# An edge-attention layer on one core: sums head by head, and more neighbour rows fetched singly

## The chip, the cores and the metric

The kernel runs on one core of a Trainium2 chip. The metric is the device time of one execution in microseconds, the median of several runs; lower is better. Engines are named as in the profile: PE (TensorE, with PEld for its weight loads), DVE (VectorE), ACT (ScalarE), POOL (GpSimd) and SP (SyncE, which here only issues DMAs).

## What is computed

There are 12500 nodes with 128 features and 412500 edges, sorted by their target `dst`, each with 64 features of its own. Attention has 4 heads of 32.

```python
h = relu(layernorm(x))                       # (12500, 128)
hn = (h @ W_node.T).reshape(N, 4, 32)
e = (edge_attr_64 @ W_edge.T).reshape(E, 4, 32)
att = sum(concat([hn[src], hn[dst], e], -1) * a, -1)      # (E, 4)
att = where(att > 0, att, 0.2 * att)
m = maximum(segment_max(att, dst), 0.0)
ex = exp(att - m[dst])
denom = segment_sum(ex, dst) + (E - deg)[:, None] * exp(-m)
out = x + segment_sum((ex / denom[dst])[..., None] * hn[src], dst)
```

The data that the layer must move one by one are the rows `hn[src]`, one for each edge.

## The kernel before

**Tiles and batches.** Edges are cut into chunks of 896 (seven tiles of 128, one edge on each partition), and seven chunks make a batch: 49 tiles in each of NBT = 66 batches; the last one has six chunks, and its last chunk three tiles. An edge's number says which chunk it is in; the targets of a chunk span fewer than 32 nodes (W = 32), so what a chunk adds up fits 32 columns or partitions.

**Preparation.** The nodes are normalised and projected in units of XB = 9 blocks of 128, and written to a table in DRAM, one row of ROW = 144 float32 (576 bytes) for a node: four heads of AW = 35 (32 values, a one that becomes the sum of the weights, another one, and the head's logit) and four more. While the table isn't there yet, POOL gathers some tiles straight from `x` (L239), and the preparation treats these "raw" tiles as it treats nodes, so that they need no row of the table. `RAW = (49, 9)` says how many in batches 0 and 1. ACT also fills the accumulator `acc` there (L453).

**Fetching.** POOL issues one indirect DMA for each tile, 128 rows of the table into `hs` (L632), in order of batches. `hs` is one of RING = 3 buffers in turn. In iteration b POOL gathers batch b+1; ahead of it stands a small memset (L627) that waits until the sums of batch b-2 have read that buffer. Some tiles are left to other queues: `by_row(b)` tiles of batch b are loaded as 128 single rows each, whose addresses the engine first reads into registers, 32 at a time, and then issues one DMA for each row (`row_by_row`, L658). The last ACTROWS = 64 rows of a batch are issued by ACT two batches ahead, at the end of an iteration; SP issues the rest, SPROWS = 96 and more in an iteration, behind its other loads: `lw` (the target rows near a chunk, `load_near`), `eft` (the edge features, L572 and L573, two batches ahead) and the penalties between segments (`load_pen`).

```python
def by_row(b):
    return (2 if b % EVERY == 0 else 1) if LOOSE < b < NBT - 1 else 0   # EVERY = 4, LOOSE = 4
```

**One iteration.** Each engine's instructions run in the order in which the program writes them; nothing reorders them. Iteration b has these steps:

- `weigh(b)`, DVE with ACT for the exponential: waits until the rows of batch b have landed (`landed`, L666), adds the logits of source and target (L734), transposes them to 32 partitions of 896 edges (L736), adds the edge's logit `z` from PSUM (L739), takes the leaky relu (L742), then the maximum of each segment by a scan forward (L745) and one backward (L748), subtracts it (L749), exponentiates on ACT (L752) and turns the weights back (L756 to L760).
- `mark(b)`: one-hot of each edge's target within its chunk (L702 to L710), `hot`.
- `scatter(b)`: DVE multiplies the rows by their weights, chunk by chunk (L774), and PE adds them up.
- `spread(b+1)` on ACT (L590) and `choose(b+1)` on DVE (L594 to L607): the target's logit of each edge, chosen from 32 rows by the bits of its number.
- `begin(b+2)`: PE's product of edge features with the attention weights into `z` (L691).
- `collect` and `close` of batch b-1: ACT copies the sums out of PSUM into `r` (L823); every second batch `merge` joins the two batches' 14 chunks in one scan along the chunks, with the running maximum, and adds the result to `acc` (L829 to L869). The last ALONE = 4 batches are merged one by one. When a part of seven blocks of nodes is complete, `finish` divides by the denominator, adds `x` and writes it out (L942 to L965); its turning of columns into rows is done by small copies on ACT (L955), or, at the very end, by products with the identity on PE (L957).

**The sums.** They are taken in two groups of four chunks (the middle chunk's heads are split between the groups), each group one chain of seven products: the weights of the product are the one-hots of four chunks, 128x128, and the moving side is 502 consecutive floats of four chunks' rows.

```python
            for t in range(T):
                at = (t * CB + q0) * ROW + g * SPLIT
                scattered[s.b] = nc.tensor.matmul(pa, s.hot[:, t, q0:q0 + G, :]..., flat[:, at:at + RUN],
                                 start=(t == 0), stop=(t == T - 1))
```

Of each result only the blocks in which a chunk's one-hot meets its own rows are used, 32 partitions of 35 columns for a head; `collect` copies these 28 blocks of a batch one by one. The last batch, with six chunks, is summed chunk by chunk (`scatter_few`, L796), and the first steps of its `weigh` are done for the tiles 0 to 4 first (EARLY = 5) and then for the other two.

## Time and profile before

| | |
|---|---|
| runs | 4023.95, 4022.22, 4022.31 us; median 4022.31 |
| profiled execution | 4021.72 us, span 4019.9 us |
| mean granted clock of TensorE | 0.678 |
| busy: PE, PEld | 1455.8 us (36%), 570.9 us (14%) |
| busy: DVE | 2373.7 us (59%) |
| busy: ACT | 865.9 us (22%) |
| busy: POOL | 3010.7 us (75%) |
| moved by DMA | 418.03 MB, 104 GB/s on average |

The span is the time from the first to the last record of the profile; the execution's own time has 1.8 us more around it. "L632 POOL" names the source line and the engine of a group of instructions; "out<-in" are the names of the tiles that it writes and reads, followed by their shapes. In groups, "x3090" counts them, and the figures behind the bar are the busy time in us, the mean duration of one in ns, and the idle time of the engine ahead of them with what ended it. In the timeline a row begins with its start and its duration in us; "x28" at its end means that so many records in a row were joined. One product in float32 leaves two records on PE.

### The profile page before, as it was taken

Reading aid. Unit: us, or ns where it says so; the run is one execution under the profiler, and the core shown is the slowest. Engines: PE = TensorE matmul, PEld = TensorE weight load, DVE = VectorE, ACT = ScalarE, POOL = GpSimd, SP = SyncE. Lnnn points to the kernel's source line nnn. Section 1 sums busy time; section 2 is a strip of 40 time slices with the busy share of each in tenths; the row PEclk is TensorE's granted clock in tenths of the full one; section 3 lists DMA queues with packets and bytes.
Section 4 is the critical chain, followed back from the end, with each engine's and each line's share of the span. In section 5 each row is a group of like instructions: output and inputs, shape, how many; then the busy total and the mean of one; then the engine's idle time right before and its main releaser. Section 6 shows DMA issues by size and latency. Waiting matters only on the chain.

```text
span 4019.9 us, 40260 instructions
## 1 busy us (share of the span) xinstructions
PE 1455.8 (36%) x3485; PEld 570.9 (14%) x3485; DVE 2373.7 (59%) x4282; ACT 865.9 (22%) x2682; POOL 3010.7 (75%) x3224
## 2 busy tenths in 40 slices
PE   5652432432442442442342442342342342343342
PEld 4320110110110110110110111110111110111111
DVE  7895565565565565465565565566465456465466
ACT  6321122112122112112122112122122122122122
POOL 6777777777777777777777777777777777777774
PEclk9776666766666666666666766676776676676676
DMA  7443333433333433433433433433334333434331
GB/s 214 130 134 109 100 96 108 110 89 99 107 91 108 110 94 99 110 87 105 109 97 95 110 88 106 108 104 88 110 89 110 104 108 85 109 89 109 109 93 42
DMA packets 283438, 418.03 MB, mean 104 GB/s; under 512 B 81019, under 2 KB 199862, under 8 KB 283146
## 3 DMA queue, kind: packets, MB, share of 16 engines
q0 software_dynamic: 100736, 231.80, 22.4%
q1 hardware_dynamic: 161232, 173.91, 14.5%
q10 hardware_dynamic: 21178, 9.69, 1.0%
q14 instruction: 262, 2.15, 0.2%
q8 instruction: 30, 0.49, 0.1%
HBM read 399.60 MB, written 15.51 MB: 103 GB/s over the span
## 4 chain that ended last, share of the span: by engine, by line
POOL 66%; issue 22%; DVE 7%; PE 3%; DMA 1%; ACT 1%; POOLq 0%; DVEq 0%; SPq 0%; ACTq 0%
POOL hs L632 66%; PE pa L781 1%; DVE hs L774 1%; PE z L691 1%; DVE stats L335 1%; DMA hs<-table,ends 1%; DVE hT L381 1%; DVE pick L607 1%; DVE m L748 0%; DVE up L745 0%; DVE hot L710 0%; DVE a L739 0%; ACT both L752 0%; DVE z L742 0%; DVE a L749 0%
## 5 line engine op out<-in xcount | busy, mean ns | idle before, releaser
L632 POOL DMA_INDIRECT hs<-table,ends x3090 | 2946.6, 954 | 945.0 <-issue 933.4
L781 PE MATMUL pa<-hs,hot 128*128 128x502 f32 x1820 | 924.6, 672 | 2428.0 <-DVE hs L774 2428.0
L734 DVE TENSOR_TENSOR logits<-hs,pick 128x196 f32<-128x196 f32 (+1 forms) x67 | 32.9, 491 | 1349.4 <-DVEq L666 1349.2
L781 PEld LDWEIGHTS pa<-hs,hot 128*128 128x128 f32 x1820 | 395.8, 222 | 2948.9 <-issue 2892.3
L823 ACT COPY r<-pa 32x35 f32<-32x35 f32 x1820 | 379.7, 209 | 1531.0 <-issue 1204.4
L774 DVE TENSOR_TENSOR hs<-hs,exr 128x924 f32<-128x924 f32 x455 | 472.5, 1110 | 0.0
L691 PE MATMUL z<-eft,wa 128*32 128x512 f32 (+3 forms) x1056 | 436.5, 549 | 13.5 <-DMA eft<-in_ef 13.5
L752 ACT ACTIVATE both<-a 32x224 f32<-32x224 f32 x264 | 102.4, 388 | 1153.1 <-DVE a L749 1150.7
L607 DVE COPY_PREDICATED pick<-exr,lw 128x3136 f32<-128x3136 int32 x66 | 239.8, 3633 | 0.0
L607 DVE COPY_PREDICATED pick<-exr,pick 128x1568 f32<-128x1568 int32 (+3 forms) x198 | 230.6, 1165 | 6.8
L590 ACT COPY pick<-lw 128x3136 f32<-128x3136 f32 x66 | 184.8, 2800 | 2.7 <-ACTq L666 1.2
L869 DVE TENSOR_TENSOR acc<-acc,a 128x70 f32 x461 | 107.2, 233 | 70.0 <-issue 51.2
L691 PEld LDWEIGHTS z<-eft,wa 128*32 128x32 f32 (+1 forms) x1056 | 94.6, 109 | 358.0 <-issue 350.7
L745 DVE TENSOR_TENSOR_SCAN up<-pen_sb,z 32x896 f32<-32x896 f32 x66 | 132.6, 2010 | 2.3
L748 DVE TENSOR_TENSOR_SCAN m<-pen_sb,up 32x896 f32<-32x896 f32 x66 | 132.5, 2007 | 2.3
L710 DVE TENSOR_TENSOR hot<-exr,key 128x448 f32<-128x448 f32 (+1 forms) x260 | 129.0, 559 | 6.7
L739 DVE TENSOR_TENSOR a<-z,zst 32x224 f32<-32x224 f32 (+2 forms) x268 | 101.0, 377 | 12.6 <-PE z L691 2.7
L756 DVE SCALAR_TENSOR_TENSOR both<-pen_sb,m 32x224 f32<-32x224 f32 x264 | 100.2, 380 | 2.7
L955 ACT COPY up<-a 32x224 f32<-32x224 f32 (+1 forms) x224 | 74.5, 332 | 36.0 <-DVE a L947 29.3
L742 DVE SCALAR_TENSOR_TENSOR z<-a 32x896 f32<-32x896 f32 (+1 forms) x67 | 72.1, 1076 | 2.3
L749 DVE TENSOR_TENSOR a<-z,m 32x896 f32<-32x896 f32 x66 | 71.3, 1080 | 2.3
L239 POOL DMA_INDIRECT hs<-in_x,ends x58 | 54.9, 947 | 18.1 <-issue 17.4
(166 smaller groups left out, 991.3 us busy)
## 6 DMA issues: line engine op xcount, KB each, us to landing
hs<-table SPq DMA_DIRECT2D x5760, 0.6 KB
eft<-in_ef SPq DMA_DIRECT2D x66, 1344.0 KB
hs<-table ACTq DMA_DIRECT2D x3840, 0.6 KB
hs<-table,ends POOLq DMA_INDIRECT x3090, 2.5
lw<-near SPq DMA_DIRECT2D x461, 64.0 KB
eft<-in_ef SPq DMA_DIRECT2D x66, 224.0 KB
pen_sb<-pens SPq DMA_DIRECT2D x66, 98.1 KB
table<-rows ACTq DMA_DIRECT2D x9, 648.0 KB
```

The costliest lines, as they stand in the source:

```text
L590: nc.scalar.copy(pick[:, :, :s.chunks, :], lw[:, None, :s.chunks, :n].to_broadcast([P, T, s.chunks, n]))
L607: nc.vector.copy_predicated(pick[:, :, :s.chunks, :n], bit[:, :, :, None].to_broadcast([P, T, s.chunks, n]), more)
L632: load = nc.gpsimd.indirect_dma_start(out=s.hs[:n, t * CB + q, :], out_offset=None, in_=table[:, :], in_offset=bass.IndirectOffsetOnAxis(a ...
L691: s.made = own_half(s, nc.tensor.matmul(s.z[:, part], wa3[:n, j, :], s.eft[:n, j, part], start=(j == 0), stop=(j == SB - 1)))
L710: nc.vector.tensor_tensor(s.hot[:, :, q0:q0 + n, :].rearrange("p t q r -> p q t r"), rows_ps[:, None, None, :].to_broadcast([P, n, T, W]), ...
L745: on_half(s, nc.vector.tensor_tensor_scan(up[:, e0:e1], s.pen[:, e0:e1], z, up[:, e0 - 1:e0] if e0 else 0.0, op0=OP.add, op1=OP.max))
L748: nc.vector.tensor_tensor_scan(m[:, ::-1], s.pen[:, CE:0:-1], up[:, ::-1], 0.0, op0=OP.add, op1=OP.max)
L752: nc.scalar.activation(both[g * R:(g + 1) * R, 0, :, :], grouped(att, g), AF.Exp)
L774: nc.vector.tensor_tensor(rows, rows, ex_ps[:, :, q * H:(q + 1) * H, None].to_broadcast([P, T, H, HB]), op=OP.mult)
L781: scattered[s.b] = nc.tensor.matmul(pa, s.hot[:, t, q0:q0 + G, :].rearrange("p q r -> p (q r)"), flat[:, at:at + RUN], start=(t == 0), sto ...
L823: nc.scalar.copy(to, pa[row:row + W, k:k + AW])
L869: nc.vector.tensor_tensor(cols, cols, put[:, i0 + i, :, :], op=OP.add)
```

## The change

It consists of six parts.

1. **Sums head by head.** `add_up` forms, for each chunk, tile and head, a product of its own: the chunk's one-hot (128x32) as weights, the 35 columns of the head as the moving side, into the 32 partitions of that head (`tile_position`) and the 35 columns of that chunk. All sums of a batch then lie in one tile of 128x245, and `collect` is one copy on ACT.
2. **DVE's steps.** `weigh_part` writes L739's sum to `up` in PSUM, makes the leaky relu out of two steps (0.2 times it into `att`, then the maximum of the two), and gives the product of the weights `up` in place of `m`. `merge` keeps `scale` and `put` in PSUM.
3. **Raw tiles.** Batch 1 gets 18 in place of 9, 67 in all. They are no longer part of the preparation: `measure_late` and `rows_late` normalise and project them in the loop, ahead of and within iteration 0. The filling of `acc` moves to iteration 1.
4. **Tiles by rows.** `by_row` gives one tile in every fourth batch and two in the others, from batch 3 to the last; ACT issues 80 or 120 rows in parts spread over its iteration (`act_some`), and SP puts 64 rows ahead of its other loads and 50 or more behind them.
5. **The last batch in two parts.** `end_in_parts` weighs, multiplies and adds up the tiles 0 to 3 of all chunks and then the tiles 4 to 6 as two segments of a chunk, which the merge joins as twelve columns.
6. **Order.** `finish` always turns by products on PE; the last batches are collected and closed in their own iteration; `mark` of the next batch comes earlier there.

```diff
-EARLY = 5
+EARLY = 4
-LOOSE = 4
-RAW = (T * CB, XB)
+LOOSE = 2
+RAW = (T * CB, 2 * XB)
-RUN = (G - 1) * ROW + SPLIT
+RUN = 512
-SPROWS = 96
-ACTROWS = 64
+SPROWS = 114
+FRONT = 64
+ACTROWS = (80, 120)
+MIDDLE = 16
+WHILE = 24

 def by_row(b):
-    return (2 if b % EVERY == 0 else 1) if LOOSE < b < NBT - 1 else 0
+    return (1 if b % EVERY == 1 else 2) if LOOSE < b < NBT else 0
+
+def act_rows(b):
+    n = ACTROWS[by_row(b) - 1] if by_row(b) else 0
+    return n if b < NBT - 2 else n * 3 // 4 if b < NBT - 1 else n // 2
...
+    def act_some(b, n):
+        if b < NBT:
+            n = min(n, batch(b).by_act)
+            batch(b).by_act -= n
+            row_by_row(batch(b), nc.scalar, ENG.Activation, n)
...
+    def weigh_part(s, t0, t1, before):
...
         for g in range(NQT):
-                on_half(s, nc.vector.tensor_tensor(grouped(att, g)[:, t0:t1, :], grouped(s.z, g)[:, t0:t1, :],
-                                                   zst[g * R:(g + 1) * R, t0:t1, :], op=OP.add))
+            on_half(s, nc.vector.tensor_tensor(grouped(up, g), grouped(s.z, g),
+                                               zst[g * R:(g + 1) * R, t0:t1, :], op=OP.add))
-            on_half(s, nc.vector.scalar_tensor_tensor(z, att[:, e0:e1], 0.2, att[:, e0:e1], op0=OP.mult, op1=OP.max))
+        nc.vector.tensor_scalar(att[:, e0:e1], up[:, e0:e1], 0.2, None, op0=OP.mult)
+        on_half(s, nc.vector.tensor_tensor(z, up[:, e0:e1], att[:, e0:e1], op=OP.max))
...
         for g in range(NQT):
             nc.vector.scalar_tensor_tensor(both[g * R:(g + 1) * R, 1, t0:t1, :], grouped(s.pen[:, 1:], g), -1.0 / BIG,
-                                           grouped(m, g), op0=OP.mult, op1=OP.mult)
+                                           grouped(up, g), op0=OP.mult, op1=OP.mult)
...
+    def add_up(s, pa, q, t0, t1):
+        for t in range(t0, t1):
+            for h in range(H):
+                scattered[s.b] = nc.tensor.matmul(
+                    pa[h * W:(h + 1) * W, q * AW:(q + 1) * AW], s.hot[:, t, q, :],
+                    s.hs[:, t * CB + q, h * AW:(h + 1) * AW],
+                    start=(t == t0), stop=(t == t1 - 1), tile_position=(0, h * W))
+
     def scatter(s):
...
+        for q in range(CB):
+            multiply(s, q, 0, T)
+            add_up(s, pa, q, 0, T)
...
     def collect(s):
...
+        nc.scalar.copy(merged[first][0][:, :, at:at + CB], s.sums)
...
+        measure_late(batch(1))
         for b in range(NBT - 1):
...
+            if b:
+                front = FRONT - row_by_row(batch(b + 1), nc.sync, ENG.SP, FRONT)
             load_near(batch(b + 1))
...
             if b:
-                more = max(SPROWS, batch(b + 1).left)
+                more = max(SPROWS - front, batch(b + 1).left)
                 more = row_by_row(batch(b + 1), nc.sync, ENG.SP, more)
                 if b + 2 < NBT:
-                    row_by_row(batch(b + 2), nc.sync, ENG.SP, min(more, max(0, batch(b + 2).left - ACTROWS)))
+                    row_by_row(batch(b + 2), nc.sync, ENG.SP, min(more, max(0, batch(b + 2).left - act_rows(b + 2))))
             weigh(s, before)
...
             scatter(s)
+            if b == 0:
+                rows_late(batch(1))
             spread(batch(b + 1))
+            act_some(b + 2, MIDDLE)
             if before:
-                close(before, b)
+                close(before, b + 2)
...
+            if b == 1:
+                nc.scalar.copy(acc.rearrange("p q d -> p (q d)"), carry_m.to_broadcast([P, NQ * AW]))
...
             if b + 2 < NBT:
                 clear_rows(batch(b + 2))
-                row_by_row(batch(b + 2), nc.scalar, ENG.Activation, ACTROWS)
+                act_some(b + 2, P)
```

`close` issues WHILE = 24 of ACT's rows between the merge and the finish of a part (`act_some(coming, WHILE)`). The functions left out of the diff are `measure_late` and `rows_late` (statistics, scaling on ACT and DVE, transposes and products with the projection on PE, a copy on ACT, for three tiles at a time) and `end_in_parts`.

More of the change, by code (lines that the diff above doesn't have):

```diff
@@ L452, in chunk_ranges @@
         def chunk_ranges():
-            nc.scalar.copy(acc.rearrange("p q d -> p (q d)"), carry_m.to_broadcast([P, NQ * AW]))
             for g in range(NG):
@@ L784, in scatter_few @@
-    def scatter_few(s, by_chunk):
-        for q in range(s.chunks):
-            rows = by_chunk[:, q, :, :].rearrange("p t (h k) -> p t h k", h=H)[:, :, :, :HB]
-            nc.vector.tensor_tensor(
-                rows, rows, ex_ps[:, :, q * H:(q + 1) * H, None].to_broadcast([P, T, H, HB]), op=OP.mult)
-            if q % G == 0:
-                pa = ps.tile([P, RUN], F32, name="pa", bufs=3)
-                s.sums.append(pa)
-            at = q % G * W
-            held = tiles_of(s.c0 + q)
-            for t in range(held):
-                nc.tensor.matmul(pa[at:at + W, :EROW], s.hot[:, t, q, :], s.hs[:, t * CB + q, :EROW],
-                                 start=(t == 0), stop=(t == held - 1), tile_position=(0, at))
+        open_weights(s)
@@ L825, in merge @@
-    def merge(c0, n, r):
+            r = work.tile([P, AW * (MC + 1)], F32, name="r")
+            merged[first] = r[:, :AW * (n + 1)].rearrange("p (d c) -> p d c", d=AW),
+        at = 1 + s.c0 - chunk_of(first)
+        nc.scalar.copy(merged[first][0][:, :, at:at + CB], s.sums)
+    def merge(c0, count, r, breaks=None):
+        n = count if breaks is None else 2 * count
+        step = n // count
+        breaks = new[:, c0:c0 + n] if breaks is None else breaks.rearrange("p c k -> p (c k)")
@@ L987, in close @@
             return
-        merge(chunk_of(first), chunks_of(first, last), merged.pop(first))
+        merge(chunk_of(first), chunks_of(first, last), *merged.pop(first))
+        if any(behind == last for _, _, behind in parts()):
+            act_some(coming, WHILE)
         for b0, n, behind in parts():
             if behind == last:
-                stores.append(finish(work, ps, "up", em_ps, b0, n, now + 1 < NBT))
+                stores.append(finish(work, ps, "up", em_ps, b0, n))
     with tc.manual_schedule():
@@ L1061 @@
                 held_x[b0] = load_part(work, b0, n)
-        for g in range(2):
-            collect(before, g)
-        weigh(s, None)
-        scatter(s)
-        close(before, NBT - 2)
-        for g in range(2):
-            collect(s, g)
-        close(s, NBT - 1)
+        merged[s.b] = end_in_parts(s)
+        close(s)
         for store in stores:
```

256 lines of the change are left out of this document (155 added, 101 removed).

## The prediction

> **What bounds the kernel now.** I read the page first, then POOL's own line, the waits, and stretches of the timeline at the start, in the middle and at the end.
>
> ```profile
> span 4019.9 us, 40260 instructions
> ...
> PE 1455.8 (36%) x3485; PEld 570.9 (14%) x3485; DVE 2373.7 (59%) x4282; ACT 865.9 (22%) x2682; POOL 3010.7 (75%) x3224
> ...
> POOL 66%; issue 22%; DVE 7%; PE 3%; DMA 1%; ACT 1%; POOLq 0%; DVEq 0%; SPq 0%; ACTq 0%
> ...
> L632 POOL DMA_INDIRECT hs<-table,ends x3090 | 2946.6, 954 | 945.0 <-issue 933.4
> ...
> L823 ACT COPY r<-pa 32x35 f32<-32x35 f32 x1820 | 379.7, 209 | 1531.0 <-issue 1204.4
> ...
> L752 ACT ACTIVATE both<-a 32x224 f32<-32x224 f32 x264 | 102.4, 388 | 1153.1 <-DVE a L749 1150.7
> ...
> L590 ACT COPY pick<-lw 128x3136 f32<-128x3136 f32 x66 | 184.8, 2800 | 2.7 <-ACTq L666 1.2
> ```
>
> POOL is busy for 75% of the span and, with the pauses called issue, makes 88% of the chain that ended last. Nearly all of it is one line, L632: 3090 gathers of 128 rows. DVE (59%), PE and ACT are far from full.
>
> ```profile
> L632 POOL DMA_INDIRECT hs<-table,ends x3090: 938/944/1822, 85.4 to 3973.5; - x194
> ```
> ```profile
> DVE logits L734 <- DVEq L666: 1349.2, 62, 29.1
> ...
> POOL hs L632 <- issue: 933.4, 3083, 0.3
> ```
>
> The first row gives POOL's pace: (3973.5 - 85.4) / 3089 = 1.259 us from gather to gather. Its median is 0.944 us, yet 2946.6 us of busy time over 3090 makes 0.954: 2946.6 - 3090 x 0.944 = 29.6 us are gathers that something held up, so an undisturbed one takes 1.259 - 0.0096 = 1.249 us. The pauses before them never exceed 0.3 us: POOL waits for nobody between 85 and 3974 us. DVE on the other hand waits 1349 us at L734 for rows, some 20 us in each of 66 batches. So the time is 85 us of start, 3090 gathers one behind the other, and a tail of 46 us.
>
> **POOL's gathers.** From the code: a batch in which by_row gives k leaves 49 - k tiles to POOL. Before, LOOSE = 4 and batches 5 to 64 give 45 x 1 + 15 x 2 = 75 tiles; after, batches 3 to 65 give 16 x 1 + 47 x 2 = 110. RAW's second entry goes from 9 to 18, so nine more tiles come from x before the table exists. POOL's gathers from the table fall from 3090 to 3046: 44 x 1.249 = 55.0 us.
>
> **The held gathers.** One batch from the middle:
>
> ```profile
> 2007.83 1.09 DVE L742 SCALAR_TENSOR_TENSOR z<-a 32x896 f32<-32x896 f32 x1
> ...
> 2008.55 1.19 POOL L632 DMA_INDIRECT hs<-table,ends  x1 [0.30 <-issue]
> ...
> 2014.05 1.56 DVE L756 SCALAR_TENSOR_TENSOR both<-pen_sb,m 32x224 f32<-32x224 f32 x4
> ...
> 2015.03 1.01 POOL L632 DMA_INDIRECT hs<-table,ends  x1 [0.30 <-issue]
> ...
> 2019.61 7.27 DVE L774 TENSOR_TENSOR hs<-hs,exr 128x924 f32<-128x924 f32 x7
> ...
> 2024.06 14.96 PE L781 MATMUL pa<-hs,hot 128*128 128x502 f32 x28 [35.84 <-DVE hs L774]
> ...
> 2030.45 24.14 ACTq L658 DMA_DIRECT2D hs<-table  x64
> ...
> 2033.14 1.83 DVE L869 TENSOR_TENSOR acc<-acc,a 128x70 f32 x7
> 2033.84 0.94 POOL L632 DMA_INDIRECT hs<-table,ends  x1 [0.31 <-issue]
> ...
> 2038.94 6.55 PE L691 MATMUL z<-eft,wa 128*32 128x512 f32 x16
> ```
>
> The gather that begins at 2008.55, while L742 runs, takes 1.19 us (+0.25), the one beside L756 1.01 (+0.07): 0.31 us in a batch, 20 us in 65 batches, of the 29.6. Both steps read two SBUF tiles; L749, L745 and L774, with z, up or ex_ps in PSUM, leave no such mark. The change puts a into PSUM as up, splits L742 into a product and a maximum with one SBUF input each, and gives L756 up in place of m. I take 22 us of the 29.6 to go (the ends are 0 and 29.6): 7.6 stay, L734 and the last copy_predicated keeping two SBUF inputs. The Trainium skill (SBUF — State Buffer, Who interferes with whom) says that a DVE instruction with two SBUF inputs contends with a GpSimd instruction that reads SBUF and that one with at most one does not; the trace agrees for L742 (1.19 us) but not for the short L869 (two inputs, 0.94 us beside it), and by the rule alone the sum would be up to 7.6 us less than by my count.
>
> **PE.** A full batch goes from 14 products of 128x502 (28 records, 14.96 us above) to 7 x 7 x 4 = 196 of 32x35, two records each: 392. Nothing of that shape is in the trace. The nearest rows:
>
> ```profile
> 4009.07 1.94 PE L957 MATMUL up<-a,ident 128*32 128x128 f32 x32 [12.01 <-DVE a L947]
> ```
> ```profile
> L796 PE MATMUL pa<-hs,eft 128*32 128x140 f32 x76 | 9.3, 337 | 26.2 <-DVE hs L788 26.2
> ```
>
> L957 has the same four column positions, with 128 columns: 1.94 / 32 = 61 ns a record, so 392 take 23.9 us at most by it, and 392 x 35/128 x 61 ns = 6.5 us if only columns count. L796 uses one position at a time and 140 columns: 9.3 / 76 = 122 ns, or 48 us. I take 12, since the positions do alternate; DVE feeds them in 7.3 us anyway. With 6.55 us for z (L691) even the dearest row gives 54.5 us against POOL's 47 x 1.249 = 58.7 in a batch, so PE stays hidden, and hs of batch b is not overwritten for two batches more. The Trainium skill (TensorEngine Tiling (Array Packing), Instruction Overhead) speaks against such small products: some 60 cycles each, whatever the columns. As an estimate from that page, with the 2.4 GHz of the Trainium skill's TensorE: Matmul & The Clock Gate (its first table), 392 x 60 cycles are 9.8 us; no run here shows it, and by it as by my 12 PE stays hidden and the sum is the same.
>
> **ACT and SP.** ACT loses 28 copies of 0.209 us for one of 128x245 (0.4 us, by the form of L590, 2800 ns for 3136), and the finish's copies by ACT, now on PE. It issues 120 rows in a two-tile batch instead of 64. 24.14 / 64 = 0.377 us a row makes 45.2 us; with L752 (102.4 / 66 = 1.6), L590 2.8, the copy 0.4 and a merge's two steps about 0.8 it is 51 of 58.7 us. The groups are smaller, which may cost up to 5 us more. SP issues about 114 rows for 93, by the same 0.377 us 43 us; 64 of them now stand ahead of lw and eft in its queue, which are wanted a batch later, so DVE's 20 us of slack hide that. The added DVE step, about 1.1 us by L742, is hidden by the same slack; if ACT or PE used it up, POOL would stand still only after another batch.
>
> **The start.**
>
> ```profile
> 74.67 0.94 POOL L239 DMA_INDIRECT hs<-in_x,ends  x1 [0.30 <-issue]
> 85.41 0.94 POOL L632 DMA_INDIRECT hs<-table,ends  x1 [9.80 <-DMA table<-rows]
> ```
> ```profile
> 86.19 11.63 ACT L453 COPY acc<-carry_m 128x13720 f32<-128x13720 f32 x1
> ```
> ```profile
> 181.81 12.05 PE L781 MATMUL pa<-hs,hot 128*128 128x502 f32 x28 [1.69 <-DVE hs L774]
> ```
> ```profile
> 199.60 0.12 POOL L627 MEMSET gate<- 128x1 f32 x1
> ```
>
> Nine more raw gathers end the raw ones at 74.67 + 9 x 1.249 = 85.9; the first from the table follows at 87.2 instead of 85.4 (+1.8). Batch 1 is left with 31, so the gate for batch 3, now at 199.6, comes at 87.2 + 80 x 1.249 + 3 = 190, and needs scatter(0), now done at 193.9. The preparation ends about 9 us earlier (three units fewer, some 4.5 us, and ACT's 11.6 us fill of acc moves to batch 1, of which I count 5), weigh(0) gains measure_late and one step, about 4 us: scatter(0) ends near 188 to 194. Then rows_late, ACT's fill and its first 120 rows (together 60 us ahead of batch 2's exp) bring scatter(2) to 300 to 322 against a gate at 307. I take 3 us of waiting on POOL in all (ends 0 and 15).
>
> **The tail.** From the rows of batch 64 on:
>
> ```profile
> 3928.51 0.50 DVE L734 TENSOR_TENSOR logits<-hs,pick 128x196 f32<-128x196 f32 x1 [18.97 <-DVEq L666]
> ...
> 3940.34 0.20 DVE L702 TENSOR_SCALAR dk<-ends 128x49 int32<-128x49 int32 x1
> ...
> 3942.87 7.27 DVE L774 TENSOR_TENSOR hs<-hs,exr 128x924 f32<-128x924 f32 x7
> ...
> 3963.78 0.20 DVE L594 TENSOR_TENSOR away<-ends,floor 128x49 int32<-128x49 int32 x1
> ...
> 3973.38 0.23 DVE L734 TENSOR_TENSOR logits<-hs,pick 128x120 f32<-128x120 f32 x1
> 3973.46 0.95 POOL L632 DMA_INDIRECT hs<-table,ends  x1 [0.31 <-issue]
> ...
> 3977.63 0.20 DVE L734 TENSOR_TENSOR logits<-hs,pick 128x48 f32<-128x48 f32 x1
> ...
> 3986.35 6.25 DVE L788 TENSOR_TENSOR hs<-hs,exr 128x924 f32<-128x924 f32 x6
> ...
> 3992.56 0.19 DVE L832 COPY run<-carry_m 128x1 f32<-128x1 f32 x1
> ...
> 3998.81 0.19 DVE L832 COPY run<-carry_m 128x1 f32<-128x1 f32 x1
> ...
> 4007.21 0.17 DVE L942 TENSOR_SCALAR rest<-acc 128x16 f32<-128x16 f32 x1
> ...
> 4011.84 0.39 SPq L965 DMA_DIRECT2D out<-xg  x1
> ```
>
> Count from E, the end of POOL's last gather (before: 3974.4, end of span E + 45.5). Batch 65 has 37 gathers by POOL, so L734 of batch 64 stands at E - 44.6. Then weigh 11.8 + 1.1, products 7.3, choose and mark of batch 65 9.6 (3963.78 to 3973.38): E - 14.8. The sums of batch 64 are there by E - 10 even at 61 ns, and its merge (6.3, from one L832 at 3992.56 to the next at 3998.81) ends near E - 5. The last batch's five-tile first steps took 4.25 us, the two-tile ones and the rest from 3977.63 to 3986.35 8.7 us: a part of four tiles costs about 8.8 us and 3.9 of products, one of three 7.6 and 2.6. E + 18; PE and one copy 2; merge of twelve columns 6.7; finish 4007.21 to 4011.84, 4.6; write and end 8.1. The span ends at E + 39.4, a gain of 6 us (ends 3 and 9).
>
> **Sum.** Last gather starts at 87.2 + 3045 x 1.249 + 7.6 + 3 = 3901.0, E = 3902.0, span 3941.4. The profiled execution took 4021.7 us for a span of 4019.9, so 3943.2; the median of the runs is 0.6 above it: 3944 us.
>
> **Rivals.** (1) The held gathers stay held, because something other than the second SBUF input holds them or the new steps fall at the same moment: +22 us, 3966. For it: L734 and L607 keep two SBUF inputs and their place shifts. Against it: L749 and L774 leave no mark. (2) The rows come late: if ACT's cycle in a two-tile batch passes 58.7 us, DVE waits at L734 for them. One us over, in 47 batches, is 47 us: 3991. Against it: one-tile batches with 80 rows give back 15 us each, and DVE has slack. (3) Slower: PE becomes the bound. If a record costs over (58.7 - 6.55) / 392 = 133 ns, scatter no longer fits. With a weight load in series at each record (570.9 / 3485 = 0.164 us by the page's PEld) a batch takes 392 x 0.164 + 6.55 = 70.8 us: 12.1 over in 47 batches and 10.9 in the others, about 4700; at 140 ns 2.7 over, 4071. Against it: 122 ns on one position alone, 61 on four. (4) The rows that replace gathers slow the other gathers, so that nothing is won: 55 / 3046 = 18 ns each would do, about 4000. Against it: gathers under ACT's and SP's rows take 0.94 us like the others.
>
> **Chances.** Forecast 0.79, (1) 0.08, (2) 0.04, (3) 0.06, (4) 0.03. A measurement of this kernel tells about 0.2% (8 us) from no change. All but (3) and a corner of (2) and (4) are faster: faster 0.90, same 0.03, slower 0.07. The range goes from 3930 (no wait in the start, no held gather, tail at its better end) to 3966 (rival 1, which is also the forecast with 15 us of waits in the start and the worse tail).
>
> **What would show it.** In the profile after: L643 x3046 with a mean near 0.946 us and first start near 87; no long gather beside the weigh steps; POOL's pauses still 0.3 us but for a few between 190 and 370 us; PE's sums of one batch between 7 and 24 us; DVE still waiting for rows in each batch; the last gather near 3901. The forecast is wrong if POOL's idle time grows by tens of us, if the new gathers' median is over 0.95, or if PE's sums pass 52 us a batch.

## The result, and the profile after

The changed kernel takes 3987.71 us (median of 4 runs, 3983.86 to 3989.80) against 4022.26 us for the kernel before: 0.9913 of it, 95% interval 0.9895 to 0.9930. It is faster by 0.9%, 34.5 us where 78 were forecast, and 3987.7 lies above the range of 3930 to 3966. The profiled execution took 3983.86 us for a span of 3982.1.

The page of the changed kernel, its first lines, the chain that ended last, and the groups that answer to those shown of before:

```profile
span 3982.1 us, 96155 instructions
...
PE 1116.7 (28%) x27848; PEld 633.4 (16%) x27848; DVE 2457.0 (62%) x4386; ACT 433.7 (11%) x693; POOL 2953.8 (74%) x3189
...
ACTq 50%; DVE 13%; SPq 13%; issue 12%; DMA 3%; ACT 3%; DVEq 0%; PE 0%
...
L643 POOL DMA_INDIRECT hs<-table,ends x3046 | 2881.1, 946 | 928.1 <-issue 919.6
L832 PE MATMUL pa<-hs,hot 128*32 128x35 f32 x25480 | 486.4, 241 | 2526.1 <-DVE hs L825 1518.2
...
L781 DVE STREAM_TRANSPOSE exr<-both 128x224 f32<-128x224 f32 (+1 forms) x67 | 28.3, 423 | 1023.9 <-ACT both L775 1023.7
```

POOL's line is what was forecast: 3046 gathers with a mean of 946 ns. But POOL is no longer in the chain that ended last. Half of that chain is ACT's queue (ACTq: the loading of row addresses and the issuing of DMAs, which don't count as busy), and the largest idle time of DVE no longer stands at the first step of a batch, where it waited for rows (L734 before, L760 now), but at L781, where it waits for ACT's exponential: 1023.7 us in 65 batches. For rows DVE waits only 1.4 us in all.

Where POOL's gathers began and ended, and POOL's and DVE's waits in the changed kernel:

```profile
L643 POOL DMA_INDIRECT hs<-table,ends x3046: 938/944/1791, 87.0 to 3910.2; - x191
```
```profile
POOL gate L638 <- PE pa L832: 8.3, 1, 8.3
POOL hs L643 <- DVE hs L631: 5.2, 1, 5.2
```
```profile
DVE exr L781 <- ACT both L775: 1023.7, 65, 29.1
...
DVE logits L760 <- DVEq L684: 1.4, 5, 0.5
```

The last gather starts at 3910.2 us and ends at 3911.2. The span ends 70.9 us after that; before, 45.5. So of the 40.7 us between the forecast's span (3941.4) and the measured one, 9.2 lie ahead of the last gather (POOL waits 8.3 us at 315 us and 5.2 us at 3885 us where 3 were counted; the gathers and the first start came out about 2 us better) and 31.5 behind it. In the timeline at the end:

```profile
3910.24 0.94 POOL L643 DMA_INDIRECT hs<-table,ends  x1 [0.30 <-issue]
...
3910.54 2.84 SPq L591 DMA_DIRECT2D lw<-near  x6
...
3917.09 2.43 ACT L600 COPY pick<-lw 128x2688 f32<-128x2688 f32 x1 [20.04 <-ACTq L684]
...
3919.55 3.13 DVE L617 COPY_PREDICATED pick<-exr,lw 128x2688 f32<-128x2688 int32 x1 [13.35 <-ACT pick L600]
...
3936.23 0.32 DVE L760 TENSOR_TENSOR logits<-hs,pick 128x96 f32<-128x96 f32 x1 [0.20 <-DVEq L684]
...
3961.01 0.36 ACT L800 COPY r<-pa 128x210 f32<-128x210 f32 x1 [5.41 <-DVE pa L815]
```

The first step of the last batch (L760 at 3936.23) begins 25 us after the end of POOL's last gather. It waited for nothing that POOL does: SP came to the loads of `lw` for this batch only at 3910.54, behind 64 single rows, DVE stood still for 13.35 us until ACT had spread what they bring (L617 behind L600), and only then could it finish with the batch before. What follows takes as long as forecast. DVE had been behind, by more or by less, all along. This is the time from the end of the last gather of a batch to the batch's first step on DVE, in us, counted from the traces (the n-th gather, with n from `by_row` and RAW); the kernels of the lower rows are those of the experiments below:

| batch | 3 | 10 | 20 | 30 | 40 | 50 | 60 | 65 |
|---|---|---|---|---|---|---|---|---|
| before | 6 | 2 | 2 | 2 | 2 | 2 | 2 | -1 |
| after | 83 | 48 | 45 | 29 | 29 | 16 | 12 | 25 |
| SPROWS = 116 (e1_fours) | 84 | 30 | 10 | 8 | 3 | 10 | 5 | -4 |
| WHILE = 0 (e2_no_while) | 83 | 55 | 63 | 52 | 55 | 60 | 68 | 12 |
| 118 tiles by rows (g5_seven_of_eight) | 84 | 45 | 46 | 55 | 55 | 39 | 52 | 24 |

A batch takes POOL 59.1 us on average, and DVE 58.25 us in the changed kernel (batches 20 to 60, from one L760 to the next). So from batch 10 on the lag of the start is worked off by less than 1 us in a batch. It goes up and down on the way (6 us at batch 57, 27 at 59, 8 at 61), and over the last four batches, which are merged one by one, it rises once more, to 33 us at batch 63; 25 are there at the end, where nothing hides them. How much of these 25 us is left from the start and how much is new isn't separated.

What holds DVE shows in ACT's timeline. Two stretches, the first of the changed kernel, the second of the same with SPROWS = 116:

```profile
2021.94 1.59 ACT L775 ACTIVATE both<-a 32x224 f32<-32x224 f32 x4 [30.82 <-issue]
...
2035.56 0.56 ACT L878 ACTIVATE up<-dif 128x462 f32<-128x462 f32 x1 [8.94 <-DVE dif L876]
...
2043.30 52.54 ACTq L669 DMA_DIRECT2D hs<-table  x104
2095.89 1.59 ACT L775 ACTIVATE both<-a 32x224 f32<-32x224 f32 x4 [59.55 <-issue]
```
```profile
2041.84 49.37 ACTq L669 DMA_DIRECT2D hs<-table  x119
2098.92 1.59 ACT L775 ACTIVATE both<-a 32x224 f32<-32x224 f32 x4 [54.69 <-DVE a L773]
```

In the first, 104 rows take 52.54 us (0.505 us a row), and the exponential follows at once, at 2095.89. DVE's own timeline of the same stretch:

```profile
2069.88 1.08 DVE L773 TENSOR_TENSOR a<-z,m 32x896 f32<-32x896 f32 x1
...
2097.51 0.43 DVE L781 STREAM_TRANSPOSE exr<-both 128x224 f32<-128x224 f32 x1 [24.96 <-ACT both L775]
```

It had the input ready at 2070.96 and stood still for 24.96 us. In the second 119 rows take 49.37 us (0.415 a row), and it is ACT that waits for DVE ("<-DVE a L773"). The chain of the changed kernel names what fills the first stretch:

```profile
2036.34 6.84 ACTq L665
...
2054.18 7.06 ACTq L665
...
2072.63 7.13 ACTq L665
```

L665 is the register load of row addresses ahead of a group of rows. Before the change they took about 2.2 us for 32 addresses; here three in a row take 7. The groups by line, before (L654) and after (L665), minimum, median and maximum in ns:

```profile
L654 ACTq TENSOR_LOAD <-shared x120: 2140/2224/3551, 279.4 to 3863.0; - x120
```
```profile
L665 ACTq TENSOR_LOAD <-shared x297: 765/2282/7439, 228.1 to 3880.9; - x149
L665 SPq TENSOR_LOAD <-shared x284: 917/2190/7172, 217.6 to 3913.7; - x142
```

### The profile page after: what moved, and what is told of

Its sections match the earlier page's. It is cut to its first block, busy times and chain, and to the rows that moved or that the text cites. A ratio compares the mean times of both kernels' runs of the same rounds, so it can differ in the third digit from the quotient of the medians.

```text
span 3982.1 us, 96155 instructions
## 1 busy us (share of the span) xinstructions
PE 1116.7 (28%) x27848; PEld 633.4 (16%) x27848; DVE 2457.0 (62%) x4386; ACT 433.7 (11%) x693; POOL 2953.8 (74%) x3189
## 4 chain that ended last, share of the span: by engine, by line
ACTq 50%; DVE 13%; SPq 13%; issue 12%; DMA 3%; ACT 3%; DVEq 0%; PE 0%
ACTq L669 34%; ACTq L665 16%; SPq L669 7%; DVE hs L825 6%; SPq L665 5%; DMA lw<-near 3%; DVE hot L728 2%; DVE pick L617 1%; ACT both L775 1%; SPq L591 1%; ACT pick L600 1%; DVE acc L905 1%; SPq L587 1%; ACT up L878 0%; DVE up L896 0%
## 5 line engine op out<-in xcount | busy, mean ns | idle before, releaser
L643 POOL DMA_INDIRECT hs<-table,ends x3046 | 2881.1, 946 | 928.1 <-issue 919.6
L832 PE MATMUL pa<-hs,hot 128*32 128x35 f32 x25480 | 486.4, 241 | 2526.1 <-DVE hs L825 1518.2
L832 PEld LDWEIGHTS pa<-hs,hot 128*32 128x32 f32 x25480 | 424.1, 146 | 2624.0 <-issue 2525.1
L781 DVE STREAM_TRANSPOSE exr<-both 128x224 f32<-128x224 f32 (+1 forms) x67 | 28.3, 423 | 1023.9 <-ACT both L775 1023.7
L825 DVE TENSOR_TENSOR hs<-hs,exr 128x924 f32<-128x924 f32 (+2 forms) x466 | 478.4, 1097 | 0.0
L775 ACT ACTIVATE both<-a 32x224 f32<-32x224 f32 (+2 forms) x268 | 103.1, 385 | 2826.6 <-issue 2729.2
L617 DVE COPY_PREDICATED pick<-exr,lw 128x3136 f32<-128x3136 int32 x66 | 240.9, 3650 | 15.2 <-ACT pick L600 15.2
L617 DVE COPY_PREDICATED pick<-exr,pick 128x1568 f32<-128x1568 int32 (+3 forms) x198 | 230.4, 1164 | 6.8
L770 DVE TENSOR_TENSOR_SCAN up<-pen_sb,z 32x896 f32<-32x896 f32 (+1 forms) x67 | 133.4, 1990 | 121.8 <-DMA pen_sb<-pens 120.6
L600 ACT COPY pick<-lw 128x3136 f32<-128x3136 f32 x66 | 184.7, 2798 | 83.9 <-ACTq L684 83.6
L905 DVE TENSOR_TENSOR acc<-acc,up 128x70 f32 x461 | 105.1, 228 | 90.2 <-issue 55.5
L772 DVE TENSOR_TENSOR_SCAN m<-pen_sb,up 32x896 f32<-32x896 f32 (+1 forms) x67 | 132.6, 1979 | 2.3
L765 DVE TENSOR_TENSOR up<-z,zst 32x224 f32<-32x224 f32 (+2 forms) x268 | 103.3, 385 | 12.8
L779 DVE SCALAR_TENSOR_TENSOR both<-pen_sb,up 32x224 f32<-32x224 f32 (+2 forms) x268 | 100.0, 373 | 3.8
L769 DVE TENSOR_TENSOR z<-up,a 32x896 f32<-32x896 f32 (+1 forms) x67 | 72.0, 1075 | 2.3
L773 DVE TENSOR_TENSOR a<-z,m 32x896 f32<-32x896 f32 (+1 forms) x67 | 71.4, 1066 | 2.3
```

Of the source, the lines that this page charges most:

```text
L600: nc.scalar.copy(pick[:, :, :s.chunks, :], lw[:, None, :s.chunks, :n].to_broadcast([P, T, s.chunks, n]))
L617: nc.vector.copy_predicated(pick[:, :, :s.chunks, :n], bit[:, :, :, None].to_broadcast([P, T, s.chunks, n]), more)
L643: load = nc.gpsimd.indirect_dma_start(out=s.hs[:n, t * CB + q, :], out_offset=None, in_=table[:, :], in_offset=bass.IndirectOffsetOnAxis(a ...
L770: on_half(s, nc.vector.tensor_tensor_scan(up[:, e0:e1], s.pen[:, e0:e1], z, 0.0, op0=OP.add, op1=OP.max))
L775: nc.scalar.activation(both[g * R:(g + 1) * R, 0, t0:t1, :], grouped(att, g), AF.Exp)
L825: nc.vector.tensor_tensor(rows, rows, ex_ps[:, t0:t1, q * H:(q + 1) * H, None].to_broadcast([P, t1 - t0, H, HB]), op=OP.mult)
```

## The experiments

The theory (A) after this: the loads that take 7 us start at a place in the list of addresses that is not a multiple of four. SPROWS = 114 leaves such places, since 114 is 2 more than a multiple of four while the other sizes are multiples of it, but for ACT's shares of the last two batches. Sorting ACT's 297 and SP's 284 loads by where they start: 32 addresses take 2.06 to 3.08 us from a multiple of four and 6.66 to 7.44 us from elsewhere; 16 take 1.2 and 3.6 to 3.9; for 32 that is 0.072 and 0.226 us an address. The rivals were (B) that the rows which ACT issues between a merge and a finish (WHILE) hold up DVE, and (C) that DVE's own work is too long to work off the start.

**e1_fours.** All sizes multiples of four.

```diff
-SPROWS = 114
+SPROWS = 116
```

> The changed kernel with SPROWS = 116 in place of 114, so that nearly every register load of row addresses starts at a multiple of four. Theory A (loads that start elsewhere cost 0.226 us a value in place of 0.072, and fill ACT's and SP's cycle to about 58 us): no load of 32 over 3.2 us, ACT's loads sum to about 560 us in place of 960, DVE's lag behind the last gather of its batch falls to under 8 us within some 20 batches, the first step of the last batch follows the last gather within 10 us in place of 25, and the time is 3955 to 3968 us. Theory B (the rows that ACT issues between merge and finish hold up DVE): the lag stays above 15 us at the end, the time above 3978. Theory C (the lag comes from the start and DVE's own work is too long to work it off): no change, 3983 to 3990.

Measured: 3942.32 us (5 runs, 3940.72 to 3943.61), 0.9796 of before (0.9783 to 0.9810). One constant gives 45 us.

```profile
L643 POOL DMA_INDIRECT hs<-table,ends x3046: 938/944/1580, 87.0 to 3897.6; - x191
```
```profile
L665 ACTq TENSOR_LOAD <-shared x312: 582/1782/5523, 227.1 to 3847.0; - x156
```
```profile
DVE logits L760 <- DVEq L684: 818.8, 49, 32.8
```
```profile
POOL 49%; issue 20%; SPq 8%; ACTq 7%; DVE 5%; DMA 3%; PE 1%; ACT 1%; DVEq 0%; POOLq 0%
```

POOL leads the chain that ended last again. Loads of 32 take 2.0 to 3.2 us but for a few in the last batches, whose shares still start off a multiple of four (up to 7.41 us). ACT's loads sum to 522 us in place of 960, DVE waits for rows again (818.8 us), the lag is down to 10 us by batch 20, and the last gather starts at 3897.6, where 3901.0 was forecast. Theory A holds; its gain was sized too low (3955 to 3968 us), because POOL's waits went too. B and C fall.

**e2_no_while.** The same rows, none between merge and finish.

```diff
-WHILE = 24
+WHILE = 0
```

> The changed kernel with WHILE = 0: ACT issues no rows between a merge and a finish, the same number of rows at the end of its iteration instead. SPROWS stays 114. Theory A: the odd starts stay, so the time stays within 8 us of 3988. Theory B: 3958 to 3972 us. Theory C: no change.

Measured: 4044.94 us (8 runs, 4022.77 to 4053.34), 1.0043 of before (1.0025 to 1.0062). None of the three had this. ACT's loads sum to 970 us, hardly more than the 960. The reason, read from the trace and not tried by itself: the 24 rows no longer fill ACT's wait for DVE between merge and finish, but stand ahead of the next exponential. Between 1069 and 2935 us ACT stands still for 75 us ahead of the finish's first step (L976), in the changed kernel for none, and ACT's queue is 63% of the chain that ended last:

```profile
ACTq 63%; DVE 15%; issue 12%; ACT 3%; SPq 1%; DVEq 1%; DMA 0%; PE 0%
```

The lag doesn't fall below 49 us before the last batch, and at the end POOL itself stands still, because DVE comes so late to clearing the last batch's incomplete tiles:

```profile
POOL hs L643 <- DVE hs L631: 61.0, 1, 61.0
POOL gate L638 <- PE pa L832: 22.1, 9, 8.0
```

So what counts is the length of ACT's chain, loads and waits together, against POOL's 58.7 us; in the changed kernel the two were about equal, and little more tips it over.

**e3_before_odd.** The kernel before, with starts at odd places.

```diff
-SPROWS = 96
+SPROWS = 95
```

> The kernel before with SPROWS = 95 in place of 96, so that many register loads start at odd places. Theory A, if the start must be a multiple of four: loads of 32 that start elsewhere take 7 us in place of 2.2, ACT's sum grows from 273 us to over 450; but DVE waits 20 us for rows in each batch, so the time stays within 8 us of 4022. If odd starts cost other than starts at 2 modulo 4, two groups of long loads are seen. Rival (long loads come from ACT and SP loading at the same time, or from the split into small groups): all loads stay at 2.0 to 3.6 us.

Measured: 4030.17 us (10 runs), 1.0016 of before (1.0007 to 1.0026).

```profile
L654 ACTq TENSOR_LOAD <-shared x135: 621/7067/7602, 282.6 to 3884.7; - x135
```

Of the loads of 32 addresses those from a multiple of four take 2.1 to 2.4 us, those from 1, 2 or 3 over one 6.6 to 7.6 us: one group of long loads, not two. ACT's sum goes from 273 to 705 us, and DVE's waits for rows hide nearly all of it: the same long loads cost 7 us here and 45 us in the changed kernel. The 7 us are those of the gathers, whose sum grows by 7.7 (2954.3 us against 2946.6).

**e4_sbuf_steps and g6_steps_on_fours.** DVE's steps as before, once in the changed kernel, once in the one with SPROWS = 116.

```diff
-            on_half(s, nc.vector.tensor_tensor(grouped(up, g), grouped(s.z, g),
+            on_half(s, nc.vector.tensor_tensor(grouped(att, g), grouped(s.z, g),
...
-        nc.vector.tensor_scalar(att[:, e0:e1], up[:, e0:e1], 0.2, None, op0=OP.mult)
-        on_half(s, nc.vector.tensor_tensor(z, up[:, e0:e1], att[:, e0:e1], op=OP.max))
+        on_half(s, nc.vector.scalar_tensor_tensor(z, att[:, e0:e1], 0.2, att[:, e0:e1], op0=OP.mult, op1=OP.max))
...
-                                           grouped(up, g), op0=OP.mult, op1=OP.mult)
+                                           grouped(m, g), op0=OP.mult, op1=OP.mult)
```

> The changed kernel with DVE's steps as before: the logits' sum in att in SBUF, the leaky relu in one step with two SBUF inputs, the product of the weights with m. If the second SBUF input holds up the gathers beside it, POOL's 3046 gathers sum to 2898 to 2905 us in place of 2881, with 1.19 us for the gather beside the leaky relu; the last gather starts 17 to 24 us later than 3910, and the time rises by 0 to 20 us, less than that because DVE's lag shrinks. If it doesn't, the sum stays within 4 us of 2881.

> The kernel with SPROWS = 116 (3942.3 us), with DVE's steps as before the change (the sum in att in SBUF, the leaky relu in one step, the weights' product with m). In the changed kernel itself the same edit made the gathers 27 us longer in all and the time 2.6 us shorter. If POOL sets the pace now, the gathers' sum grows by 25 to 29 us over 2879.6 and the time by as much: 3962 to 3970 us. If the time stays within 8 us of 3942, POOL isn't what sets it.

Measured: 3985.10 us (4 runs, 3983.17 to 3986.90) for the first, the same as the changed kernel within the spread of the runs, where a rise of 0 to 20 us was expected, and 3966.13 us (4 runs, 3964.40 to 3969.05) for the second, 23.8 more than without the edit. The gathers, first of e4, then of g6:

```profile
L643 POOL DMA_INDIRECT hs<-table,ends x3046 | 2908.2, 955 | 923.7 <-issue 918.5
```
```profile
L643 POOL DMA_INDIRECT hs<-table,ends x3046 | 2905.4, 954 | 927.3 <-issue 923.4
```

In both the gathers grow by 26 to 27 us, and the last one of e4 starts at 3929.7, 19 us later than without the edit. It costs time only where POOL sets the pace. In the changed kernel itself the gain of this part was real on POOL and worth nothing.

**g8_while_on_fours.** WHILE = 0 with SPROWS = 116.

> The kernel with SPROWS = 116 (3942.3 us) with WHILE = 0. With SPROWS = 114 the same edit cost 57 us. If ACT's chain only has to stay under POOL's pace: with the loads at multiples of four ACT has some 7 us a batch to spare, and the move costs some 10 us in one batch of four to five, so the time stays within 6 us of 3942, the lag at the end under 12 us. If it still rises by 20 us or more, the rows' place costs by itself, whatever the loads take.

Measured: 3952.28 us (4 runs, 3951.21 to 3956.57), 10 more than e1_fours, between the two answers. The last gather starts at 3898.9, 1.3 us later than in e1_fours: POOL's pace isn't touched, so in the long run the place of the rows costs nothing while ACT has time to spare. The other 7.5 us of the span lie behind it: the lag is 11 us at batch 64 and 4 at the last, against 2 and -4. Why the last batches come later is open.

**g7_rows_on_fours and g9_raw_on_fours.** The price of a gather, with SPROWS = 116.

```diff
-    return (1 if b % EVERY == 1 else 2) if LOOSE < b < NBT else 0
+    return (2 if b % EVERY == 0 else 1) if LOOSE < b < NBT - 1 else 0
-LOOSE = 2
+LOOSE = 4
```
```diff
-RAW = (T * CB, 2 * XB)
+RAW = (T * CB, XB)
```

> The kernel with SPROWS = 116 (3942.3 us) with by_row and LOOSE as before the change: 75 tiles by rows in place of 110, 3081 gathers. If a gather is worth POOL's 1.249 us: 35 x 1.249 = 43.7, 3982 to 3990 us, and DVE waits for rows some 20 us in a batch again. If rows slow the gathers beside them, the mean gather falls below 0.944 us and the time stays under 3980.

> The kernel with SPROWS = 116 (3942.3 us) with RAW's second entry at 9 as before, still worked on in the loop: nine gathers are moved behind the table, not removed. The first gather from the table then waits for the table, at 82 to 86 us, and the end comes 6 to 11 us later, 3948 to 3954, if POOL's queue alone counts. If DVE's and PE's work on the first batches limits the start, the time stays within 4 us of 3942.

Measured: 3981.08 us (4 runs) with 75 tiles by rows, 38.8 more than with 110; the last gather starts at 3940.1, 42.6 later, 1.22 us for each of the 35. That is 1 us under the 3982 to 3990 expected; the mean gather stays at 946 ns, so the rows don't slow it. With nine raw tiles less 3946.72 us (4 runs), 4.4 more, between the two answers: POOL waits 9.8 us for the table, as before the change, so most of what the nine raw gathers take was a gap that POOL had anyway.

**g5_seven_of_eight and g10_five_of_six.** More tiles by rows, 118 and 116 in place of 110.

```diff
-EVERY = 4
+EVERY = 8
-SPROWS = 116
+SPROWS = 120
-ACTROWS = (80, 120)
+ACTROWS = (80, 124)
```
```diff
-EVERY = 4
+EVERY = 6
-SPROWS = 116
+SPROWS = 120
-ACTROWS = (80, 120)
+ACTROWS = (80, 128)
```

> The kernel with SPROWS = 116 (3942.3 us) with two tiles by rows in seven of eight batches (EVERY = 8, SPROWS = 120, ACTROWS = (80, 124)), 118 in place of 110. If POOL still sets the pace: 8 gathers less, 10 us, 3930 to 3935 us. ACT then issues some 116 rows a batch, 116 x 0.343 + 8.5 of loads + 5 of its own work = 53 us of 58.7, and SP 118 rows, 118 x 0.33 + 10 + 7.5 of other issues = 56; if waits inside these two chains fill the rest, DVE lags again by 20 us or more at the end and the time is 3942 to 3970 us.

> The kernel with SPROWS = 116 (3942.3 us) with two tiles by rows in five of six batches, 116 in place of 110, SPROWS = 120 and ACTROWS = (80, 128), so that ACT issues 7488 rows and SP 7360 (in the run with 118 tiles 7389 and 7715). If SP's chain was what ran over there: SP has 117 rows a batch, 117 x 0.33 + 9 + 7.5 = 55 us, ACT 119, 119 x 0.343 + 8.7 + 5.2 = 55 us, both under 58.7; POOL sets the pace, six gathers less, 3932 to 3937 us. If ACT's was it, ACT is as full as there, DVE lags by 40 us or more and the time is over 3980 us.

Measured: 4052.52 us (5 runs) with 118, 110 more than with 110 tiles and far over both answers; 3945.56 us (5 runs, 3942.16 to 3947.23) with 116, over the 3932 to 3937 expected. ACT issues 7389 rows in the first and keeps up with 7488 in the second, SP has 7715 and 7360: it was SP's chain that ran over. The trace of the first agrees: SP's queue leads the chain that ended last, and DVE's wait for ACT (818.8 us at L781) has behind it ACT's own wait for the `lw` that SP issues late:

```profile
SPq 35%; ACTq 22%; issue 14%; DVE 13%; DMA 7%; ACT 2%; DVEq 1%; PE 0%
```
```profile
ACT pick L600 <- ACTq L684: 301.9, 47, 19.1
```

In the first DVE never catches up, and POOL waits at the end:

```profile
POOL hs L643 <- DVE hs L631: 82.4, 1, 82.4
```

In the second the last gather starts at 3895.2, 2.4 earlier than in e1_fours, for six gathers less, and the span ends 49.3 us after that gather's end, against 42.0: nothing more was won. The best of all these is e1_fours, 3942.3 us, which beats both kernels.

**Eight runs with slow rows.** e5_seven_of_eight, e6_steps_on_fours, e7_rows_on_fours and e9_raw_on_fours, and once more the first three with f8_while_on_fours (f5 to f8), are the kernels of g5 to g9. Where they ran, the kernel before takes 6505 to 6524 us, so they can't be compared with the others. The record gives chip 0 for the first four and chip 5 for the rest, and chip 5 for g5, g7 and g9 as well, beside which the kernel before takes 4024 us. What was expected, largely in the same words as for g5 to g9:

> The kernel with loads at multiples of four (SPROWS = 116 took 3942.3 us) with one more tile by rows: two tiles in seven of eight batches (EVERY = 8, SPROWS = 120, ACTROWS = (80, 124)), 118 in place of 110. If POOL still sets the pace: 8 gathers less, 10 us, 3930 to 3935 us. ACT then issues some 116 rows a batch, 116 x 0.343 + 8.5 of loads + 5 of its own work = 53 us of 58.7, and SP 118 rows, 118 x 0.33 + 10 + 7.5 of other issues = 56; if waits inside these two chains fill the rest, DVE lags again by 20 us or more at the end and the time is 3942 to 3970 us.

> The kernel with SPROWS = 116 (3942.3 us), with DVE's steps as before the change (the sum in att in SBUF, the leaky relu in one step, the weights' product with m). In the changed kernel itself the same edit made the gathers 27 us longer in all and the time 2.6 us shorter. If POOL sets the pace now, the gathers' sum grows by 25 to 29 us over 2879.6 and the time by as much: 3962 to 3970 us. If the time stays within 8 us of 3942, POOL isn't what sets it.

> The kernel with SPROWS = 116 (3942.3 us) with by_row and LOOSE as before the change: 75 tiles by rows in place of 110, 3081 gathers. If a gather is worth POOL's 1.249 us: 35 x 1.249 = 43.7, 3982 to 3990 us, and DVE waits for rows some 20 us in a batch again. If rows slow the gathers beside them, the mean gather falls below 0.944 us and the time stays under 3980.

> The kernel with SPROWS = 116 (3942.3 us) with RAW's second entry at 9 as before, still worked on in the loop: nine gathers more from the table, the first of them 11 us earlier. The nine are moved, not removed: if POOL's one queue sets the time, what counts is only that raw gathers run before the table is there; then the first gather from the table waits for the table, at 82 to 86 us, and the end comes 6 to 11 us later, 3948 to 3954. If the start was limited by DVE's and PE's work on the first batches, the time stays within 4 us of 3942.

> The kernel with loads at multiples of four (SPROWS = 116 took 3942.3 us) with more tiles by rows: two tiles in seven of eight batches (EVERY = 8, SPROWS = 120, ACTROWS = (80, 124)), 118 in place of 110. If POOL still sets the pace: 8 gathers less, 10 us, 3930 to 3935 us. ACT then issues some 116 rows a batch, 116 x 0.343 + 8.5 of loads + 5 of its own work = 53 us of 58.7, and SP 118 rows, 118 x 0.33 + 10 + 7.5 of other issues = 56; if waits inside these two chains fill the rest, DVE lags again by 20 us or more at the end and the time is 3942 to 3970 us.

> The kernel with SPROWS = 116 (3942.3 us), with DVE's steps as before the change (the sum in att in SBUF, the leaky relu in one step, the weights' product with m). In the changed kernel itself the same edit made the gathers 27 us longer in all and the time 2.6 us shorter. If POOL sets the pace now, the gathers' sum grows by 25 to 29 us over 2879.6 and the time by as much: 3962 to 3970 us. If the time stays within 8 us of 3942, POOL isn't what sets it.

> The kernel with SPROWS = 116 (3942.3 us) with by_row and LOOSE as before the change: 75 tiles by rows in place of 110, 3081 gathers. If a gather is worth POOL's 1.249 us: 35 x 1.249 = 43.7, 3982 to 3990 us, and DVE waits for rows some 20 us in a batch again. If rows slow the gathers beside them, the mean gather falls below 0.944 us and the time stays under 3980.

> The kernel with SPROWS = 116 (3942.3 us) with WHILE = 0. With SPROWS = 114 the same edit cost 57 us, because ACT's chain was already as long as POOL's and the 24 rows left a wait that they had filled. With the loads at multiples of four ACT has some 7 us a batch to spare, and the move costs some 10 us in one batch of four to five: the time stays within 6 us of 3942, the lag at the end under 12 us. If it still rises by 20 us or more, the rows' place costs by itself, whatever the loads take.

None of it was met: 7318 to 7330 us with 118 tiles by rows, 7104 to 7143 with 110, and 6282 to 6293 with 75. Their ratios to before are 1.124 and 1.126 with 118 tiles by rows, 1.092 to 1.096 with 110, and 0.964 and 0.966 with 75. What is slow there is the issuing of single rows (f7; SP's queue, then ACT's):

```profile
3025.82 146.11 SPq L669 DMA_DIRECT2D hs<-table  x116
...
3190.09 16.89 SPq L669 DMA_DIRECT2D hs<-table  x48
```
```profile
3118.11 74.22 ACTq L669 DMA_DIRECT2D hs<-table  x81
...
3194.69 34.10 ACTq L669 DMA_DIRECT2D hs<-table  x55
```

116 rows take 1.26 us each and 48 rows 0.35 us each, and ACT issues rows beside both. Counted over the whole run, 36% of SP's rows start more than 0.6 us after the one before while ACT is issuing too and 6% while it isn't; of ACT's rows 37% and 24%. So slow rows are more frequent where both queues issue, but issuing together isn't enough for them, and some come without it. What makes them slow, and whether it is the chip, is open.

## Why the prediction was wrong

The step that failed is the cost of the queues in the part on ACT and SP: "24.14 / 64 = 0.377 us a row makes 45.2 us ... it is 51 of 58.7 us", with "up to 5 us more" for smaller groups, and for SP "by the same 0.377 us 43 us". The 0.377 holds one load of 2.2 us for 32 rows, as every load of before had. After the change the median load is no longer than that (2.28 us), but 126 of ACT's 297 start off a multiple of four, and one of 32 addresses then takes 7.2 us. Between the first steps of batches 16 and 48 (1865.9 us, 58.3 us a batch) ACT issued 3511 rows at 0.343 us (1204 us), made 152 loads (494 us) and worked 165 us itself: 1863 us; in the same stretch with SPROWS = 116 it is 3520 rows, 1211 + 264 + 165 = 1640. So a cycle that was put at 51 us for a batch with two tiles, and less with one, was 58 on average.

The sum has some overlap, since copies run while rows are issued: pauses over 0.3 us between ACT's instructions add up to 109 us of the stretch, 55 of them for the merge's step on DVE and 37 for `lw`; with SPROWS = 116 they are 341. SP's queue, put at 43 us by its rows alone, was fuller still: its pauses are 27 of the 1866 us, with SPROWS = 116 106. e1_fours shortens both queues at once, so how much of the 45 us belongs to each isn't separated; e2_no_while lengthens ACT's chain alone and g5 mainly SP's, and either is enough to hold DVE. With that DVE's 20 us of slack were gone, on which the same part let SP's 64 rows stand ahead of `lw`: at the last batch DVE waits 13.35 us behind them.

- **The gathers**: right. 3046 from 87.0 us, and 1.22 us saved for each that goes (g7), 1.249 forecast.
- **The held gathers**: right. Of 2881.1 us, 3046 x 0.944 leaves 5.7 held (7.6 forecast); the old steps bring back 26 us of gathers, and 23.8 us of time where POOL sets it (g6), 22 forecast. The Trainium skill (SBUF — State Buffer, Who interferes with whom) agrees: the edit brings back the two steps with a second SBUF input, and the held gathers with them. It also makes one step of two, which wasn't tried apart.
- **PE**: right that it stays hidden; 486.4 us for 65 batches are 7.5 us a batch, below the 12 taken.
- **The start**: POOL waited 8.3 us there, not 3 (the 5.2 us come at 3885 us, where DVE clears tiles late). What was missed is what it stands for: DVE was 83 us behind at batch 3 (before: 6), and only a cycle shorter than POOL's works that off.
- **The tail**: from the last batch's first step to the end 45.9 us, by the forecast's own terms 44.4 (from E - 5 to E + 39.4). But that step came at E + 25.
- **The sum**: with the loads mended it comes out: e1_fours takes 3942.3 us against 3944, its last gather starts at 3897.6 against 3901.0, and its span ends 42.0 us after that gather's end, against 39.4.
- **The rivals**: (2), with a chance of 0.04, comes nearest, since it has ACT's cycle reach POOL's 58.7 us. But its wait isn't the one that came: DVE waits 1.4 us for rows (L760) and 1023.7 us for an exponential that stands behind the rows in ACT's queue (L781). Nor is its price: it takes a cycle over 58.7 us, where one equal to it is enough, since then the lag of the start isn't worked off. That its 3991 us lie near the measured 3988 is luck. (1), (3) and (4) did not come: the held gathers went, PE is hidden, and the other gathers kept their 944 ns.
- **The signs**: of the three that were to show the forecast wrong none came (POOL's idle time, the gathers' median, PE's sums); all look at POOL and PE. The one that did fail is "DVE still waiting for rows in each batch".

Not settled is what a load from elsewhere does in its 7 us: the runs show the two prices only. Nor was the new way of summing tried alone, since it shares its tiles with the new `collect` and merge, nor the last batch in two parts.

## What to carry to other kernels

A queue that is written out by hand has a length of its own, and where another engine waits for something that stands in it, that length has to fit the cycle: add up every instruction in it, address loads and waits too, by its form and not by the mean of a different pattern, before putting more on it. A lag that is built up at the start costs nothing until the end, and is worked off only by the difference of the two paces; look at the lag by batch, not at busy shares. A gain on the bound engine and one hidden by a new bound look the same in that engine's own line (e4), so price each part again once the bound is mended (g6).

## What the runs showed of the hardware

- A load of 32 addresses into registers takes 2.0 to 3.2 us (0.072 us an address in the changed kernel) when it starts at a multiple of four 4-byte words in its row, and 6.6 to 7.6 us (0.226 us) when it starts at 1, 2 or 3 over one (the changed kernel, e1, e3), on ACT and SP alike. A load of 16 takes 1.2 and 3.6 to 3.9 us.
- A product of 128x32 weights with 35 columns, the four column positions in turn, keeps PE busy for 19 ns a record on average (486.4 us / 25480), where 128 columns in four positions take 61 (L957 before) and 140 columns in one position 122 (L796 before). A product of float32 leaves two records, so it is 38 ns. The Trainium skill (TensorEngine Tiling (Array Packing), Instruction Overhead) gives some 60 cycles each, an estimate of 25 ns at the 2.4 GHz of its page TensorE: Matmul & The Clock Gate: more than a record took here and less than a product, and no run here shows which of the two it counts.
- Single rows from SP's and ACT's queues together take 0.33 to 0.34 us each in some runs, and up to 1.26 us each for a whole group in others (f7) of the same kernel (g7); what sets this is open.
